# Half-row transposes in the projection's tiling, and the next columns' transposes at the head of a step

## The chip, the core and the metric

One core of a Trainium2 chip runs the whole program. The metric is device time in microseconds (us), the median of several runs; lower is better. The engines are TensorE (PE; its weight loads are shown apart as PEld), VectorE (DVE), ScalarE (ACT), GpSimd (POOL) and SyncE (SP), which here only issues DMAs.

## What is computed

An image x of 512 x 512 pixels with 64 channels goes through two layers of the same form. All data are fp32. Cut to what matters:

```python
def conv(x):                       # one layer; L = 512, H = 128 hidden channels
    xn = layernorm(x)              # over the 64 channels
    left = (xn @ Wl) * mask * sigmoid(xn @ Wlg)
    right = (xn @ Wr) * mask * sigmoid(xn @ Wrg)
    gate = sigmoid(xn @ Wog)
    # banded: out[i, j] = sum over d in -4..4 of left[i + d, i] * right[i + d, j], channel by channel
    out = banded_ingoing(left, right, 4)
    return (layernorm(out) * gate) @ Wo

for _ in range(2):
    x = x + conv(groupnorm(x))     # groupnorm: 32 groups, statistics over all pixels
```

(Biases are added too; they are left out here.)

## The kernel before, in words

Rows are cut into nine blocks of 64 rows that overlap by eight; columns into units of eight columns. A unit holds, on the 128 partitions, the 64 rows of a block twice: the lower 64 partitions have eight columns of the left half of the image, the upper 64 eight columns of the right half. A chunk is 16 units (JC = 128 columns in each half), and a layer has 18 chunks, so 288 units, plus five units of columns near the diagonal for `left`, early in the layer.

`layer` (L674) is one loop over steps t, and in a step each part works on another unit. Every call through `en` is kept in program order on its engine, so the order in which the loop writes things is the order in which each engine does them. In a step, in this order:

- GpSimd applies groupnorm's scale and shift to a unit some seven steps ahead (`affine`, L415; two operations, z<-z,ga and z<-z,gb).
- `gates` (L594): TensorE multiplies the stored transposed rows (zg) by the gate's weights, twice 64 rows by 448 columns; ScalarE takes the sigmoid into two gate tiles.
- `right` (L459), twice: `projected` (L447) multiplies the transposed unit zT by the weights into a tile of two PSUM banks, each matmul using 64 of the 128 rows of the array, with the two halves of the image in the two row tiles; ScalarE takes a sigmoid (sg), VectorE multiplies the two into RO.
- `inner_norm` (L424) of unit t+2 on GpSimd (z<-z,sti and z<-z,rs).
- `transposed` (L430) of unit t+1: four transposes of 128 x 128 into one PSUM bank, then ScalarE copies the bank to zT and SyncE stores zT to `later`, from where `recall` (L590) brings it back as zg some 30 steps on.
- `turned` (L613): eight transposes of 128 x 128 of the normed mix `on`, four into each of two banks; VectorE adds, multiplies by the gate and writes ZH.
- `biased` (L637) on GpSimd, then `end` (L643) of the step before: the output projection from ZH on TensorE, a VectorE addition into XR and the output's DMAs. In layer 0, `sums` (L662) accumulates the next groupnorm's statistics (acc).
- In every fourth step `solve` (L549): VectorE prepares var and rs, GpSimd works out the reciprocal roots by Newton steps, for four units to come.
- `norm` (L582): eight ScalarE activations from RO to `on`, of which there is one buffer.
- `mix` (L511), none, one or two times a step: 32 matmuls on 64 x 64 tiles into two banks; the banks are copied back into RO by ScalarE (first half) and ScalarE or VectorE (second half). Of 16 steps the first ten have 2, 1, 2, 2, 1, 2, 1, 2, 2, 1 mixes, the last six none (L695).

PSUM is shared out by two pools: `two_banks` (L131) has two buffers and serves `projected` and `mix`; `one_bank` (L128) has three buffers in layer 0 and four in layer 1 (L899) and serves transposes, gates and output. A user of a buffer waits until the one before it has been read out. zT has two buffers, sg two, z twelve.

Of the kernel before, what the change touches and what calls it, by code (L numbers as in the profile page):

```python
# [8 lines left out]
F32 = mybir.dt.float32  # L9
I32 = mybir.dt.int32  # L10
AF = mybir.ActivationFunctionType
ALU = mybir.AluOpType
# [4 lines left out]
P = 128  # L17
WIN = 4
NEAR = 2 * WIN + 1
S = 64  # L20
JC = 128
JW = 16
JU = 8
JQ = 4
NU = JC // JU
# [54 lines left out]
def tile_two_banded_layers(  # L80
# [8 lines left out]
    H = layers[0]["Wl"].shape[1]  # L89
    x, out = x[0], out[0]  # L90
# [22 lines left out]
    ident = const.tile([P, P], F32, name="ident")  # L113
# [14 lines left out]
    def one_bank():  # L128
        return ps.tile([P, 512], F32, tag="ps", name="bank")

    def two_banks():  # L131
        return ps2.tile([P, 1024], F32, tag="ps2", name="banks")
# [30 lines left out]
    def views(pack: bass.AP) -> dict:  # L163
        r, at = {}, 0
        for nm, n in PARTS:
            r[nm] = pack[:, at : at + n]
            at += n
        return r
# [184 lines left out]
    w = views(pack)  # L353
# [75 lines left out]

    def transposed(u: Unit):  # L430

        u.t = ztp.tile([P, JU // 2, P], F32, tag="zT", name="zT")
        pt = one_bank()
        for k in range(JU // 2):
            en.tensor.transpose(
                pt[:, k * P : (k + 1) * P],
                u.z[:, 2 * k : 2 * k + 2, :].rearrange("p j c -> p (j c)"), ident,
            )
        en.scalar.activation(u.t.rearrange("c k p -> c (k p)"), pt, AF.Identity, bias=1.0)
        if u.near is None:  # L440
            en.sync.dma_start(later[u.at], u.t)

    def place(k: int, e: int) -> int:

        return k // 2 * 4 + 2 * e + k % 2
# [147 lines left out]

    def gates(o: Out, w: dict):  # L594
        b = o.blk
        o.g = []
        pgs = [
            one_bank()[:, : 2 * JQ * b.m].rearrange("h (k p) -> h k p", p=b.m) for e in range(2)
        ]
        for e, pg in enumerate(pgs):  # L600
            part = slice(e * D, (e + 1) * D)
            en.tensor.matmul(
                pg, lhsT=w["gate"][part],
                rhs=o.t[part].rearrange("c k (e p) -> c (k e) p", e=2)[:, :, b.lo : b.hi],
                start=True, stop=True,
            )
        for pg in pgs:
            g = gp.tile([H, 2 * JQ * (S - WIN)], F32, tag="gate", name="gate")
            g = g[:, : 2 * JQ * b.m].rearrange("h (k p) -> h k p", p=b.m)
            en.scalar.activation(g, pg, AF.Sigmoid)  # L610
            o.g.append(g)

    def turned(o: Out, w: dict):  # L613

        b = o.blk
        for e in range(2):
            pt = one_bank()
            for k in range(JQ):
                en.tensor.transpose(
                    pt[:, k * P : (k + 1) * P], o.on[:, place(k, e), :], ident  # L620
                )
            zh = ZH[(2 * o.n + e) % len(ZH)]
            en.vector.scalar_tensor_tensor(
                zh[:, :, : b.m], pt.rearrange("h (k p) -> h k p", p=S)[:, :, b.lo : b.hi], w["ob"], o.g[e],
                ALU.add, ALU.mult,
            )

    def rows_of(v: bass.AP, o: Out, e: int):
        b, j = o.blk, e * LH + o.j
        return v[b.s + b.lo : b.s + b.hi, j : j + JU, :].rearrange("p (k t) c -> p k (t c)", t=2)  # L630
# [12 lines left out]
    def end(dst: bass.AP, o: Out, w: dict):  # L643
        m = o.blk.m
        po = one_bank().rearrange("i (j c) -> i j c", c=D)
        for k in range(JQ):
            for e in range(2):
                for n in range(2):

                    en.tensor.matmul(  # L650
                        po[n * S : (n + 1) * S, 2 * k + e, :],
                        lhsT=ZH[(2 * o.n + e) % len(ZH)][:, 2 * k + n, :], rhs=w["Wo"],
                        start=True, stop=True,
                    )
        f = o.xr[: S + m, :, 1 : 1 + 2 * D]
        en.vector.tensor_tensor(
            f, po[: S + m].rearrange("i (k t) c -> i k (t c)", t=2), f, ALU.add
        )
        for e in range(2):
            en.sync.dma_start(rows_of(dst, o, e), o.xr[e * S : e * S + m, :, 1 : 1 + 2 * D])  # L660
# [13 lines left out]
    def layer(src: bass.AP, dst: bass.AP, w: dict, stats: bool, then=None):  # L674
# [6 lines left out]
        for c in range(n_chunks):  # L681
            b, t0 = blocks[c // per], (c + 1) * NU
            for k in range(NU):
                t = c * NU + k
                units[t] = u = Unit(t, blk=b, j=c % per * JC + k * JU)
                j = k * JU if c % 2 == 0 else (JC + k * JU if k < own else JC - JW + (k - own) * JU)
                u.c = j

            for f in range(NU):
                o = outs[c * NU + LAG + f] = Out(  # L690
                    b, units[c * NU + (f + own) % NU], c % per * JC + f * JU
                )
# [9 lines left out]
        for n in range(0, NEAR * JQ, JU):  # L702
            t = 3 + n // JU * 2
# [3 lines left out]
        def inputs(t: int) -> list:  # L707
            return [d[t] for d in (units, lefts) if t in d]
# [22 lines left out]
        for t in range(min(loads), last_t + 3):  # L731
            if then and t == max(units) + 2:
                then()
            for u in loads.get(t, []):
                if u not in early:
                    load(src, u)
            if t + 2 in outs:
                recall(outs[t + 2])
            if t + 1 in outs:
                fetch(src, outs[t + 1], w, t + 1)  # L740
            for c, h in slabs.get(t, []):
                A[c, h] = take_left(c // per, h)

            for o in looks.get(t, []):
                if sto is None:
                    sto = sm.tile([P, NB // 2, 6], F32, tag="sto", name="sto"), []
                st, os = sto
                for k in range(JU // 2):
                    out_stats(o, st[:, len(os) * (JU // 2) :], k)
                os.append(o)  # L750

            for u in affines.pop(t, []):
                affine(u, en.vector if u.at < NU + 4 else en.gpsimd)
            if t % 4 == 3 and t > NU:
                then_affine = affines.pop(t + 1, [])
            if t in outs:
                gates(outs[t], w)

            todo = []
            for at, u in inners.get(t, []):  # L760
                key = (at + 2) // 4
                if key not in sti:
                    sti[key] = sm.tile([P, 3 * NB // 4, 6], F32, tag="sti", name="sti", bufs=3), []
                st, us = sti[key]
                n = len(us) * (JU // 2)
                u.mean = st[:, n : n + JU // 2, 1::3]
                todo += [(u, st[:, n : n + JU // 2, :], k) for k in range(JU // 2)]
                us.append(u)
            for v in todo[: len(todo) // 2]:
                inner_stats(*v)  # L770
            if t in units:
                for q in range(0, JU, JQ):
                    right(units[t], q, w)
            if t in lefts:
                for q in range(0, min(JU, NEAR * JQ - lefts[t].near), JQ):
                    left(lefts[t], q, w)
            for u in inputs(t + 2):
                inner_norm(u)
            for u in inputs(t + 1):
                transposed(u)  # L780
            if t in outs:
                turned(outs[t], w)
                biased(outs[t], w, stats)
            for v in todo[len(todo) // 2 :]:
                inner_stats(*v)
            if t - 1 in outs:
                end(dst, outs[t - 1], w)
            if stats and t - 2 in outs:
                sums(outs[t - 2], t - 2 == first_t, t - 2 == last_t)
            if t % 4 == 3:  # L790
                st, us = sti.pop((t + 5) // 4, (None, []))
                so, os = sto or (None, [])
                sto = None
                for u in then_affine:
                    affine(u, en.gpsimd)
                then_affine = []
                if us or os:
                    solve(w, us, os, st, so)
            if t + 1 in outs:
                norm(outs[t + 1])  # L800
            for n, (c, h0) in enumerate(mixes.get(t, [])):
                mix(c, A[c, h0 // HA], h0, [True, n + 1 < len(mixes[t])])
# [77 lines left out]
    ZH = [keep.tile([H, 2 * JQ, S], F32, name=f"ZH{i}") for i in range(4)]  # L880
# [9 lines left out]
    lp = ctx.enter_context(tc.tile_pool(name="lp", bufs=NA))  # L890
    wk = ctx.enter_context(tc.tile_pool(name="wk", bufs=3))
    onp = ctx.enter_context(tc.tile_pool(name="onp", bufs=1))
    gp = ctx.enter_context(tc.tile_pool(name="gp", bufs=2))

    next(one, None)
    nc.sync.dma_start(pack, spare)
# [35 lines left out]
```

## Time and profile before

| what | value |
|---|---|
| median of 3 runs | 5074.97 us (5073.14 to 5075.13) |
| the profiled execution | 5074.14 us, span 5072.3 us |
| granted TensorE clock in it | 0.978 |
| TensorE busy | 4496.1 us, 89% |
| VectorE, ScalarE, GpSimd busy | 3732.8, 3793.8 and 3826.9 us (74 to 75% each) |
| transposes of z, 128 x 128, 2344 in number | 390.6 us, 128.8 us idle ahead of them |
| transposes of on, 128 x 128, 4608 in number | 616.6 us, 14.7 us idle ahead of them |
| evictions to zT, 586 in number | 350.1 us, 597 ns each |

Each instruction is named by its output and inputs, such as bank<-ident,z for the transposes of z, banks<-pack,zT for the projection, banks<-RO,A for the mix, bank<-zg,pack for the gates and bank<-pack,ZH for the output projection. All of them carry the line of the one wrapper that records them (L362), so they are told apart by name. A number after an arrow is time in which the engine stood idle just before such instructions, with the engine that released it. An fp32 matmul is two records, a transpose one. Ends of matmuls are modelled, so it is the distance between starts that says what TensorE takes.

### The profile page before, as it was taken

How to read it: one execution, taken by the hardware profiler on the slowest of the kernel's cores; microseconds unless marked ns; L12 is line 12 of the kernel's file. 1: busy time of each engine (PE TensorE's matmuls, PEld its weight loads, DVE VectorE, ACT ScalarE, POOL GpSimd, SP SyncE). 2: the span in 40 equal slices, each digit the busy share in tenths (PEclk: the TensorE clock that was granted, in tenths of full speed). 3: DMA queues.
4: the chain of work that ended last, by engine and by line, in shares of the span. 5: the costliest groups of instructions: out<-in, count | busy, mean ns of one | idle time of the engine just before them, and what ended most of it. 6: DMA issues, size and time to landing. Idle time of an engine off the chain costs nothing.

```text
span 5072.3 us, 159784 instructions
## 1 busy us (share of the span) xinstructions
PE 4496.1 (89%) x60138; PEld 3714.8 (73%) x60138; DVE 3732.8 (74%) x9445; ACT 3793.8 (75%) x8328; POOL 3826.9 (75%) x4739
## 2 busy tenths in 40 slices
PE   1027999999999999999995599999999999999999
PEld 0015788888888888888873478888888888888886
DVE  6764677777777777777766467777777777777776
ACT  0013788888888888888884268888888888888888
POOL 0037888888888888888733598888888888888863
PEclk9988999999999999999997799999999999999999
DMA  7924666666666666666663456767676776777766
GB/s 317 400 58 125 176 194 197 195 195 193 198 196 195 194 194 197 196 194 198 189 171 102 106 176 201 202 198 202 200 205 201 202 203 200 202 204 204 204 182 173
DMA packets 905291, 981.45 MB, mean 193 GB/s; under 512 B 114210, under 2 KB 641608, under 8 KB 900168
## 3 DMA queue, kind: packets, MB, share of 16 engines
q1 hardware_dynamic: 897248, 948.49, 63.5%
q10 hardware_dynamic: 7272, 22.73, 1.1%
q8 instruction: 477, 7.82, 0.7%
q14 instruction: 294, 2.41, 0.2%
HBM read 658.42 MB, written 312.46 MB: 191 GB/s over the span
## 4 chain that ended last, share of the span: by engine, by line
PE 72%; POOL 9%; DMA 6%; DVE 4%; ACT 3%; issue 2%; SPq 2%; another core or an unknown queue 0%; ACTq 0%; POOLq 0%; DVEq 0%
PE banks L362 38%; PE bank L362 32%; POOL z L362 6%; ACT on L362 2%; DMA left_of<-nothing 2%; PE acc L362 2%; SPq L362 2%; DVE RO L362 1%; POOL XR L362 1%; DMA gn_x<-in_x_dram 1%; POOL rsqrt L362 1%; DVE ZH L362 1%; DMA XR<-mid_x 1%; DVE sto L362 1%; ACT gate L362 1%
## 5 line engine op out<-in xcount | busy, mean ns | idle before, releaser
L362 ACT ACTIVATE on<-RO,nm,rs 128x128 f32<-128x128 f32 x4608 | 1879.2, 495 | 172.4 <-PE bank L362 169.9
L362 PE MATMUL banks<-pack,zT 64*128 64x256 f32 x9360 | 1213.1, 389 | 137.0 <-ACT zT L362 76.6
L362 PEld LDWEIGHTS banks<-pack,zT 64*128 64x128 f32 x9360 | 967.2, 192 | 419.8 <-issue 180.4
L362 PE MATMUL banks<-RO,A 64*64 64x128 f32 x18432 | 1154.5, 277 | 15.6 <-DVE RO L362 15.4
L362 PEld LDWEIGHTS banks<-RO,A 64*64 64x64 f32 x18432 | 1082.4, 183 | 43.6 <-DVE RO L362 18.6
L362 DVE TENSOR_TENSOR RO<-banks,sg 128x512 f32<-128x512 f32 x1152 | 747.0, 681 | 258.8 <-ACT sg L362 258.0
L362 ACT ACTIVATE sg<-banks 128x512 f32<-128x512 f32 (+1 forms) x1188 | 682.7, 589 | 319.8 <-PE banks L362 208.0
L362 DVE COPY RO<-banks 128x512 f32<-128x512 f32 x360 | 248.9, 692 | 869.1 <-ACT RO L362 869.1
L362 DVE BATCH_NORM_STATS2 sto<-RO 128x6 f32<-128x256 f32 x2304 | 797.5, 411 | 1.2
L362 DVE SCALAR_TENSOR_TENSOR ZH<-bank,pack,gate 128x448 f32<-128x448 f32 (+1 forms) x1152 | 740.0, 682 | 37.6 <-ACT gate L362 36.3
L362 POOL TENSOR_TENSOR z<-z,gb 128x512 f32<-128x512 f32 x536 | 687.7, 1283 | 42.1
L362 POOL TENSOR_TENSOR z<-z,ga 128x512 f32<-128x512 f32 x536 | 687.5, 1283 | 0.1
L362 PE MATMUL bank<-zg,pack 64*128 64x448 f32 (+1 forms) x2304 | 657.4, 595 | 18.9 <-DVE ZH L362 15.8
L362 PE MATMUL bank<-pack,ZH 128*64 128x64 f32 x18432 | 663.5, 225 | 2.8 <-ACT zT L362 0.3
L362 ACT ACTIVATE gate<-bank 128x448 f32<-128x448 f32 (+1 forms) x1152 | 567.1, 542 | 126.6 <-PE bank L362 125.8
L362 PEld LDWEIGHTS bank<-pack,ZH 128*64 128x64 f32 x18432 | 584.0, 138 | 100.3 <-ACT zT L362 83.2
L362 POOL TENSOR_TENSOR z<-z,rs 128x512 f32<-128x512 f32 x586 | 618.0, 1055 | 45.9
L362 PE MATMUL bank<-ident,on 128*128 128x128 f32 x4608 | 616.6, 274 | 14.7 <-ACT gate L362 12.1
L362 POOL TENSOR_TENSOR z<-z,sti 128x512 f32<-128x512 f32 x586 | 623.8, 1065 | 0.0
L362 ACT COPY RO<-banks 128x512 f32<-128x512 f32 x792 | 441.2, 586 | 239.0 <-PE banks L362 237.8
L362 PEld LDWEIGHTS bank<-ident,on 128*128 128x128 f32 x4608 | 519.7, 141 | 74.0 <-ACT on L362 24.3
L362 POOL TENSOR_TENSOR XR<-XR,pack 120x512 f32<-120x512 f32 (+1 forms) x352 | 418.4, 1189 | 192.4 <-DMA XR<-mid_x 90.4
(137 smaller groups left out, 3927.6 us busy)
## 6 DMA issues: line engine op xcount, KB each, us to landing
later<-zT SPq DMA_DIRECT2D x576, 256.0 KB
A<-left_of SPq DMA_DIRECT2D x576, 256.0 KB
zg<-later SPq DMA_DIRECT2D x576, 256.0 KB
z<-in_x_dram SPq DMA_DIRECT2D x576, 128.0 KB
z<-mid_x SPq DMA_DIRECT2D x576, 128.0 KB
gn_x<-in_x_dram SPq DMA_DIRECT2D x16, 4096.0 KB
XR<-in_x_dram SPq DMA_DIRECT2D x448, 112.0 KB
mid_x<-XR SPq DMA_DIRECT2D x448, 112.0 KB
```

The costliest lines, as they stand in the source:

```text
L362: return lambda *a, **k: tc.keep_in_program_order(f(*a, **k))
```

## The change

Five things change, and nothing in the arithmetic.

1. `transposed` works on half rows: eight transposes instead of four, each of 64 partitions by 128 columns against a 64 x 64 part of the identity. The two halves of the partitions go to two different PSUM banks. For most units both come from one `two_banks` tile; for the first 17 units of a layer and the five near the diagonal they are two `one_bank` tiles.
2. Its eviction is a function of its own, `kept`: one activation over both banks (or two, for two tiles), which puts the halves together in zT, and the DMA to `later`.
3. Both are called for unit t+1 ahead of `gates` and `right` of step t, no longer after `right`.
4. `turned` works on half rows as well: sixteen transposes instead of eight, the halves in two banks, both evicted after the last transpose.
5. The gate is one tile of twice the size with one buffer, instead of two tiles with two, and ZH is indexed by half instead of by e.

```diff
     def transposed(u: Unit):
+        if u.near is None and u.at > NU:
+            u.pt = [two_banks().rearrange("c (n x) -> c n x", n=2)[:, :, : JU // 2 * S]]
+            halves = [u.pt[0][:, n] for n in range(2)]
+        else:
+
+            halves = [one_bank()[:, : JU // 2 * S] for n in range(2)]
+            u.pt = [h.unsqueeze(1) for h in halves]
+        for k in range(JU // 2):
+            for n in range(2):
+                part = slice(n * S, (n + 1) * S)
+                en.tensor.transpose(
+                    halves[n][:, k * S : (k + 1) * S],
+                    u.z[part, 2 * k : 2 * k + 2, :].rearrange("p j c -> p (j c)"),
+                    ident[part, part],
+                )
+
+    def kept(u: Unit):
         u.t = ztp.tile([P, JU // 2, P], F32, tag="zT", name="zT")
-        pt = one_bank()
-        for k in range(JU // 2):
-            en.tensor.transpose(
-                pt[:, k * P : (k + 1) * P],
-                u.z[:, 2 * k : 2 * k + 2, :].rearrange("p j c -> p (j c)"), ident,
-            )
-        en.scalar.activation(u.t.rearrange("c k p -> c (k p)"), pt, AF.Identity, bias=1.0)
+        to = u.t.rearrange("c k (n p) -> c n k p", n=2)
+        for n, pt in enumerate(u.pt):
+            en.scalar.activation(
+                to[:, n : n + pt.shape[1]], pt.rearrange("c n (k p) -> c n k p", p=S),
+                AF.Identity, bias=1.0,
+            )
         if u.near is None:
             en.sync.dma_start(later[u.at], u.t)
...
     def turned(o: Out, w: dict):
 
         b = o.blk
+        pts = [one_bank().rearrange("h (x p) -> h x p", p=S) for n in range(2)]
         for e in range(2):
-            pt = one_bank()
             for k in range(JQ):
-                en.tensor.transpose(
-                    pt[:, k * P : (k + 1) * P], o.on[:, place(k, e), :], ident
-                )
-            zh = ZH[(2 * o.n + e) % len(ZH)]
+                for n, pt in enumerate(pts):
+                    part = slice(n * S, (n + 1) * S)
+                    en.tensor.transpose(
+                        pt[:, e * JQ + k, :], o.on[part, place(k, e), :], ident[part, part]
+                    )
+        for n, pt in enumerate(pts):
             en.vector.scalar_tensor_tensor(
-                zh[:, :, : b.m], pt.rearrange("h (k p) -> h k p", p=S)[:, :, b.lo : b.hi], w["ob"], o.g[e],
-                ALU.add, ALU.mult,
+                ZH[(2 * o.n + n) % len(ZH)][:, :, : b.m], pt[:, :, b.lo : b.hi], w["ob"],
+                o.g[:, n], ALU.add, ALU.mult,
             )
...
             if t % 4 == 3 and t > NU:
                 then_affine = affines.pop(t + 1, [])
+            for u in inputs(t + 1):
+                transposed(u)
+                kept(u)
             if t in outs:
                 gates(outs[t], w)
...
             for u in inputs(t + 2):
                 inner_norm(u)
-            for u in inputs(t + 1):
-                transposed(u)
             if t in outs:
                 turned(outs[t], w)
...
-    gp = ctx.enter_context(tc.tile_pool(name="gp", bufs=2))
+    gp = ctx.enter_context(tc.tile_pool(name="gp", bufs=1))
```

More of the change, by code (lines that the diff above doesn't have):

```diff
@@ L595, in gates @@
         b = o.blk
[L596 to L599, printed above, removed]
+        n = 2 * JQ * b.m
+        pgs = [one_bank()[:, :n].rearrange("h (k p) -> h k p", p=b.m) for e in range(2)]
         for e, pg in enumerate(pgs):
@@ L606, in gates @@
             )
[L607 to L611, printed above, removed]
+        g = gp.tile([H, 4 * JQ * (S - WIN)], F32, tag="gate", name="gate")
+        for e, pg in enumerate(pgs):
+            en.scalar.activation(
+                g[:, e * n : (e + 1) * n].rearrange("h (k p) -> h k p", p=b.m), pg, AF.Sigmoid
+            )
+        o.g = g[:, : 2 * n].rearrange("h (x n p) -> h n x p", n=2, p=b.m)
     def turned(o: Out, w: dict):
         b = o.blk
+        pts = [one_bank().rearrange("h (x p) -> h x p", p=S) for n in range(2)]
         for e in range(2):
-            pt = one_bank()
             for k in range(JQ):
-                en.tensor.transpose(
-                    pt[:, k * P : (k + 1) * P], o.on[:, place(k, e), :], ident
-                )
-            zh = ZH[(2 * o.n + e) % len(ZH)]
+                for n, pt in enumerate(pts):
[4 more added lines that the diff above has]
+        for n, pt in enumerate(pts):
             en.vector.scalar_tensor_tensor(
-                zh[:, :, : b.m], pt.rearrange("h (k p) -> h k p", p=S)[:, :, b.lo : b.hi], w["ob"], o.g[e],
-                ALU.add, ALU.mult,
+                ZH[(2 * o.n + n) % len(ZH)][:, :, : b.m], pt[:, :, b.lo : b.hi], w["ob"],
+                o.g[:, n], ALU.add, ALU.mult,
             )
@@ L651, in end @@
                         po[n * S : (n + 1) * S, 2 * k + e, :],
-                        lhsT=ZH[(2 * o.n + e) % len(ZH)][:, 2 * k + n, :], rhs=w["Wo"],
+                        lhsT=ZH[(2 * o.n + n) % len(ZH)][:, e * JQ + k, :], rhs=w["Wo"],
                         start=True, stop=True,
```

## The prediction

> **What bounds the kernel now.** I read the page's busy slices first, then the table by stretches, then the timeline of TensorE and GpSimd inside one stretch.
>
> ```profile
> PE 4496.1 (89%) x60138; PEld 3714.8 (73%) x60138; DVE 3732.8 (74%) x9445; ACT 3793.8 (75%) x8328; POOL 3826.9 (75%) x4739
> ...
> PE   1027999999999999999995599999999999999999
> ```
>
> TensorE is full in every slice except the set-up and the two starts of a layer; the other four engines stand near 75%. But an average mixes stretches. A chunk of 16 steps (124.9 us in layer 0, 121.1 in layer 1) has ten steps with mixes and six without. The table by stretches, for one chunk of layer 0 (us; busy PE, PEld, DVE, ACT, POOL; clock, DMA share, GB/s):
>
> ```profile
> 1937.69:2016.37 78.68, 78.68 (x1170) 67.95 (x1169) 52.87 (x136) 63.78 (x136) 70.99 (x80) 1.00 0.67 190
> 2016.37:2035.41 19.04, 18.37 (x242) 15.22 (x240) 18.19 (x49) 16.34 (x36) 9.73 (x17) 1.00 0.67 195
> 2035.41:2052.90 17.49, 17.28 (x244) 13.87 (x240) 15.08 (x39) 16.62 (x40) 16.94 (x17) 1.00 0.72 212
> ```
>
> Mix steps: TensorE 78.68 of 78.68. The first three steps without a mix: VectorE 18.19 of 19.04. The last three: GpSimd 16.94 of 17.49. So three engines take turns, and TensorE is only just slower than GpSimd in the last stretch. The timeline there (start, length), TensorE and then GpSimd:
>
> ```profile
> 2035.41 1.02 PE L362 MATMUL bank<-zg,pack 64*128 64x448 f32 x4
> 2036.27 1.89 PE L362 MATMUL banks<-pack,zT 64*128 64x256 f32 x16
> 2038.14 0.66 PE L362 MATMUL bank<-ident,z 128*128 128x128 f32 x4
> 2038.64 1.04 PE L362 MATMUL bank<-ident,on 128*128 128x128 f32 x8
> 2039.63 1.15 PE L362 MATMUL bank<-pack,ZH 128*64 128x64 f32 x32
> 2040.61 0.64 PE L362 MATMUL acc<-XR 120*64 120x65 f32 x16
> 2041.18 1.02 PE L362 MATMUL bank<-zg,pack 64*128 64x448 f32 x4
> ```
> ```profile
> 2031.38 0.29 POOL L362 TENSOR_TENSOR rsqrt<-rs 128x64 f32<-128x64 f32 x1 [4.56 <-DVE rs L362]
> ...
> 2035.92 1.05 POOL L362 TENSOR_TENSOR z<-z,sti 128x512 f32<-128x512 f32 x1
> 2037.05 1.04 POOL L362 TENSOR_TENSOR z<-z,rs 128x512 f32<-128x512 f32 x1
> ```
>
> GpSimd's normalisation ends at 2038.09 and the transposes of z start at 2038.14: they wait for it. What covers that wait today are the gates and the projection of the same step, issued ahead (2035.41 to 2038.14). In the next two steps it is the same (z at 2044.02 and 2049.90, 5.88 us apart: GpSimd's 2.13 + 1.14 + 2.61 for norm, bias, affine).
>
> **What the Trainium skill says.** "TensorEngine Tiling (Array Packing)", Key Properties: changing the tiling mode drains the array. The trace agrees: the last pair of the projection takes 0.306 instead of its 0.216, and the first transpose 0.165 instead of 0.109. "TensorE: Matmul & The Clock Gate", section LDWEIGHTS: a load costs by columns, not by rows. The trace differs, and decides:
>
> ```profile
> L362 PEld LDWEIGHTS banks<-pack,zT 64*128 64x128 f32 x9360 | 967.2, 192 | 419.8 <-issue 180.4 <-ACT zT L362 96.8 <-DVE RO L362 50.3
> ...
> L362 PEld LDWEIGHTS bank<-ident,on 128*128 128x128 f32 x4608 | 519.7, 141 | 74.0 <-ACT on L362 24.3 <-ACT gate L362 20.8 <-ACT RO L362 14.1
> ```
>
> The same 128 columns read 51 ns longer in a 64-row tile; single records agree (an exposed load delays the first matmul by 0.104 at the gates, 0.056 at z). The same page, Part 3: loads overlap if their row groups differ. At the gates both halves' loads start 7 ns apart, so two run together.
>
> **The change, part by part.** Times per step, from the single records.
> (1) Tiling. Now, from the end of a mix to the output projection: gates 0.86 (0.104 exposed load, two pairs at 0.376), projection 1.82, z 0.49, the on-transposes 0.97: 4.14. After: z first, 0.104 + 4p, gates 0.75, projection 1.73, on 8p + 0.09, where p is the time of a pair of half transposes: 2.67 + 12p. One change of mode (0.09 + 0.056) is gone, and the gates' load hides under z. p is not in the trace. Below: the load alone, 0.104; above: 0.121, the pair pitch of the mix (3.87 us for 32 pairs), which streams the 128 columns that cost 0.109 untiled. Were both loads serial, 0.21, but the gates speak against it. I take 0.115: 4.05, a gain of 0.09 (0.22 to 0.02).
> (2) z moves into two_banks, and the built order shows that after a mix the projection's first bank is the one that z just left, so it waits for zT. ScalarE: copy of the mix from 0.12 to 0.71 after the mix, zT to about 1.34, seen at 1.40. TensorE would be there at 0.10 + 4 x 0.115 + 0.75 = 1.32. Cost about 0.06 to 0.08, leaving a gain of 0.03 per mix step, 10 x 0.03 = 0.3 per chunk (1.5 to -0.5). In layer 1 a step with one mix lasts 7.25, less than the 7.55 after which ScalarE ends its eight activations on; there zT comes some 0.2 later, in three steps: 0.6.
> (3) z is moved ahead of gates and projection. In mix steps z has been ready for long (3.4 to 11 us for most; 1.6 to 2.5 in the first two steps). In the last three steps the cover of 2.7 us is taken off. Layer 0: z cannot start before 2038.13; then the whole step follows it, 5.69 - 0.09 = 5.60, to 2043.73; z ready at 2043.97; 2049.57, ready at 2049.84; then 2055.44, where the mix step begins today at 2052.90: 2.5 late. GpSimd gets nothing back for it: its own chain starts at VectorE's rs (2031.4), which ends an unbroken VectorE run from the last mix. Step 1 gains nothing in these six steps, as VectorE and GpSimd set them. ScalarE's sum is 5.9 per step (zT 0.6, gates 0.95, sg 1.05, on 3.25), so zT behind on adds about 0.2. Layer 0: 2.5 + 0.2 - 0.3 = 2.4 per chunk. Layer 1: the same recurrence with 5.22 per step gives 2.5; but there the mix stands waiting for VectorE 1.3 in the next step, which swallows that much; the step after has z 1.7 before its use against 2.7 of lost cover and so waits 0.4; with 0.6 of (2), less 0.3: 1.9.
> (4) Half rows in the first 17 units: two activations (128x256 at 0.381) for one of 0.597, 0.17 each, ScalarE half idle there: nothing, 4 us if not. turned now evicts after all sixteen instead of eight: at worst 0.5 late for VectorE, which is read a step later: nothing. gp with one double tile: the gate's sigmoid waits for the ZH of the step before, done by then. SP: later is issued 2.7 earlier and still ahead of the output; the queue behind it waits for zT a shorter time. GpSimd's order is unchanged. The two ends: steps without a projection save about 0.12 in 28 steps per layer, 7 together. Starts of the layers: zT now stands ahead of sg in ScalarE's queue, where today sg waits 96 us for left_of and zT 53 us for later; zT being ready when the wait ends could save 3 in some of eight places, and its own wait now holds sg: between -25 and +15, taken -10.
>
> Sum: 16 chunks with such stretches per layer: 16 x 2.4 + 16 x 1.9 = 69, less 7 and 10: 52. On the profiled execution (span 5072.3, 1.8 around it, time 5074.1) 5126; that one stands 0.8 under the median of the runs, so 5127.
>
> **The rivals.** A, faster: p at its lower bound and the starts at theirs. Then a mix step gains 0.15 after its wait, 1.5 per chunk, against 2.2 left of step 3: +0.7 x 32 = 22, minus 7, minus 25, minus what the earlier z saves VectorE's stretch (gates there wait 0.4 to 0.6 for ZH, twice; z would fill it): 20 if VectorE follows. In all -30: 5045. It decides once step 3 costs less than ten gains of step 1, that is below 0.15 per mix step. For it: the gates' loads run in parallel; against: VectorE is full in that stretch, and the mix never reaches 0.109. B, no change: a gain of 0.18 per mix step instead of 0.03 (p near its lower bound, zT early), the rest as forecast: 52 - 32 x 10 x 0.15 = +4, 5079. C, clearly slower: zT's eviction becomes the bound in every mix step: ScalarE's queue puts it after the copy, and each 0.1 beyond costs 32 x 10 x 0.1 = 32; at 0.3 more: 5222.
>
> **How the numbers follow.** Forecast 0.56 (own range 5095 to 5165), A 0.19, B 0.10, C 0.15. The range 5055 to 5200 leaves out about half of A and a third of C. This kernel's measurement can tell about 0.2%, 10 us. Faster 0.19, within 0.2% 0.11 (B and the edge), slower 0.70.
>
> **What would show it.** Right: in the last three steps without a mix, TensorE idle 2 to 4 us ahead of the first z, released by GpSimd, and nothing between z and the end of the step; waits of TensorE for z up by about 70 us or more; VectorE's stretch unchanged; pairs of halves 0.105 to 0.121 apart; the projection after a mix held by zT for under 0.1. Wrong: chunk periods at or below 124.9 and 121.1; pairs below 0.10 or above 0.15; or GpSimd's solve starting earlier in the chunk, which would mean that VectorE's run was shortened.

## The result and the profile after

| | before | after |
|---|---|---|
| median, same series of runs | 5073.14 us | 5099.26 us (5094.57 to 5104.45) |
| ratio | | 1.0055, 95% interval 1.004 to 1.0069 |
| the profiled execution | 5074.14 us | 5100.56 us, span 5098.6 us |
| granted clock in it | 0.978 | 0.927 |

The changed kernel is 26 us slower; 52 were forecast. Direction and range held, but the sum did not: two of its terms were wrong by about a hundred and by about seventy-five, with opposite signs. The page after, its busy line of TensorE and the busy slices:

```profile
PE 4296.7 (84%) x67090; PEld 3572.6 (70%) x67090; DVE 3696.4 (72%) x9445; ACT 3793.5 (74%) x8372; POOL 3821.5 (75%) x4739
...
PE   1025899999999999999984479999999999999998
```

TensorE has 200 us less to do and the kernel is slower. The slices that differ are at the start (0258 where it was 0279) and in the middle, where layer 1 starts (4479 where it was 5599). So one looks there first.

The places where a mix begins are easy to find in the trace (banks<-RO,A), and they cut a layer into comparable stretches. "Mix stretch" is from a chunk's first mix to its last, "gap" from there to the first mix of the next chunk, both medians over the steady chunks; worked out from the starts of the records, in us:

| kernel | median | first mix | mix stretch of chunk 0 | layer 0: mix, gap | last mix of layer 0 to first of layer 1 | layer 1: mix, gap |
|---|---|---|---|---|---|---|
| before | 5073 | 460.8 | 57.5 | 80.6, 44.4 | 280.2 | 76.3, 44.8 |
| after | 5099 | 477.9 | 67.9 | 76.4, 47.1 | 299.5 | 72.8, 46.7 |
| start_old | 5045 | 461.0 | 58.1 | 76.4, 47.1 | 278.7 | 72.9, 46.7 |
| nomix_old | 5049 | 477.7 | 68.0 | 77.3, 44.7 | 301.1 | 75.3, 43.6 |
| both_old | 4986 | 458.6 | 58.1 | 77.8, 43.9 | 279.1 | 73.7, 44.8 |
| on_halves | 5016 | 461.2 | 58.1 | 79.5, 44.2 | 282.0 | 74.3, 43.7 |
| serial_on | 5218 | 480.6 | 65.7 | 79.1, 48.3 | 302.7 | 75.1, 47.7 |
| move_only | 5318 | 481.2 | 61.2 | 81.9, 50.5 | 301.1 | 77.7, 48.0 |
| tiling_only | 5459 | 461.8 | 64.1 | 86.1, 50.1 | 277.9 | 82.5, 50.4 |
| start_bank | 5083 | 475.9 | 60.0 | 76.4, 47.1 | 297.3 | 72.8, 46.7 |
| late_head | 4960 | 459.4 | 57.5 | 76.7, 44.1 | 279.8 | 74.3, 43.6 |

The ledger of the two profiled executions, from the first two rows and the starts behind them: layer 0 up to the first mix of its second chunk +31.6; its next sixteen chunks -21.3; from there to the first mix of layer 1 +20.2, and to the first of its second chunk +14.9; sixteen chunks -16.6; the last chunk -2.4. Sum 26.4. Steady chunks became faster, by 1.3 and 1.0 us each in the mean (1.5 and 1.6 by the medians of the table, since single chunks of layer 1 differ), where 2.4 and 1.9 slower were forecast. The two starts of a layer lost 67, where 10 of gain were forecast.

Inside a steady chunk of layer 0, the table by stretches of the changed kernel (us; busy PE, PEld, DVE, ACT, POOL; clock, DMA share, GB/s), cut as in the prediction:

```profile
1955.16:2029.68 74.52, 74.52 (x1282) 63.69 (x1280) 53.44 (x136) 63.84 (x137) 68.35 (x78) 1.00 0.73 202
2029.68:2051.64 21.96, 17.09 (x282) 14.37 (x280) 20.21 (x55) 17.65 (x40) 13.87 (x22) 0.98 0.74 209
2051.64:2068.94 17.30, 17.30 (x281) 14.20 (x279) 12.52 (x30) 15.44 (x36) 15.71 (x15) 0.93 0.51 145
```

Mix steps 78.68 to 74.52; the next three steps 19.04 to 21.96, with TensorE busy only 17.09 of them; the last three as long as before. The idle time is one wait. TensorE and then GpSimd there:

```profile
2046.91 0.64 PE L362 MATMUL acc<-XR 120*64 120x65 f32 x16
2051.16 0.69 PE L362 MATMUL banks<-ident,z 64*128 64x64 f32 x8 [3.62 <-POOL z L362]
2051.64 1.81 PE L362 MATMUL bank<-zg,pack 64*128 64x448 f32 x4
2053.24 2.32 PE L362 MATMUL banks<-pack,zT 64*128 64x256 f32 x16
...
2057.54 0.47 PE L362 MATMUL banks<-ident,z 64*128 64x64 f32 x8
```
```profile
2044.41 0.29 POOL L362 TENSOR_TENSOR rsqrt<-rs 128x64 f32<-128x64 f32 x1 [4.34 <-DVE rs L362]
...
2048.94 1.05 POOL L362 TENSOR_TENSOR z<-z,sti 128x512 f32<-128x512 f32 x1
2050.07 1.04 POOL L362 TENSOR_TENSOR z<-z,rs 128x512 f32<-128x512 f32 x1
...
2055.91 1.04 POOL L362 TENSOR_TENSOR z<-z,rs 128x512 f32<-128x512 f32 x1
```

GpSimd ends the normalisation at 2051.11, and z starts at 2051.16 after 3.62 of idleness; the gates and the projection, which used to fill that time, now follow it. GpSimd's roots begin 14.7 after the last mix (2044.41 less 2029.68), 15.0 before the change (2031.38 less 2016.37): VectorE's stretch is nearly unchanged. All this is as forecast, but for one thing: the z of the next step has no wait. GpSimd has it ready at 2056.95 (2055.91 and 1.04), about as forecast, but TensorE comes to it only at 2057.54, because its own step took 6.38 and not 5.60. The step after the wait ran at a lower granted clock (the value before the DMA share):

```profile
2051.16:2053.24 2.08, 2.08 (x12) 1.27 (x14) 0.00 (x0) 0.60 (x1) 2.08 (x2) 0.50 0.07 20
```

At 0.50, z takes 0.48 here and the gates 1.60, where a mix step has 0.30 and 0.96 (below). The clock records of the traces show 0.50 for 3.4 or 6.8 us in the gap of each of the 32 steady chunks of the changed kernel, and in none of them in before, nomix_old and late_head, which do not have this long wait. By this, the lost cover costs twice: the wait, and the slow step behind it. No run separates the two; in this chunk the second z starts 0.59 after it is ready.

A mix step, on TensorE and then ScalarE:

```profile
1971.22 0.46 PE L362 MATMUL banks<-ident,z 64*128 64x64 f32 x8
1971.52 0.97 PE L362 MATMUL bank<-zg,pack 64*128 64x448 f32 x4
1972.48 2.00 PE L362 MATMUL banks<-pack,zT 64*128 64x256 f32 x16
1974.31 0.66 PE L362 MATMUL bank<-ident,on 64*128 64x64 f32 x16
1974.90 0.28 PE L362 MATMUL bank<-pack,ZH 128*64 128x64 f32 x2
```
```profile
1971.34 0.58 ACT L362 COPY RO<-banks 128x512 f32<-128x512 f32 x1 [0.76 <-PE banks L362]
1971.83 0.60 ACT L362 ACTIVATE zT<-banks 128x512 f32<-128x512 f32 x1
```

From start to start: z 0.30 (was 0.49), gates 0.96 (0.86), projection 1.83 (1.82), on 0.59 (0.97). The sum is 3.68 instead of 4.14, and a step with two mixes is 9.10 instead of 9.56. The projection starts 0.05 after zT ends (1971.83 + 0.60): the wait for zT that was forecast is there; its size follows from both_old below. What was not forecast is how short the transposes are: eight pairs of on take 0.438 from first to last start, which is 0.062 a pair. The records of their loads (busy, mean ns of one | idle before):

```profile
L362 PEld LDWEIGHTS bank<-ident,on 64*128 64x128 f32 x9216 | 413.9, 139 | 126.3 <-ACT gate L362 40.0 <-issue 17.3 <-DVE XR L362 8.0
```

### The profile page after: what moved, and what is told of

Read it like the earlier page. It is cut to its first block, busy times and chain, and to the rows that moved or that the text cites. A ratio compares the mean times of both kernels' runs of the same rounds, so it can differ in the third digit from the quotient of the medians.

```text
span 5098.6 us, 172846 instructions
## 1 busy us (share of the span) xinstructions
PE 4296.7 (84%) x67090; PEld 3572.6 (70%) x67090; DVE 3696.4 (72%) x9445; ACT 3793.5 (74%) x8372; POOL 3821.5 (75%) x4739
## 4 chain that ended last, share of the span: by engine, by line
PE 65%; POOL 8%; DMA 7%; DVE 7%; ACT 6%; SPq 3%; issue 3%; ACTq 0%; another core or an unknown queue 0%; POOLq 0%; DVEq 0%
PE banks L362 40%; PE bank L362 23%; POOL z L362 4%; ACT on L362 3%; SPq L362 3%; POOL rsqrt L362 3%; DMA left_of<-nothing 2%; PE acc L362 2%; DVE RO L362 2%; DVE ZH L362 2%; DMA gn_x<-in_x_dram 1%; DVE sti L362 1%; ACT gate L362 1%; DMA zg<-later 1%; ACT sg L362 1%
## 5 line engine op out<-in xcount | busy, mean ns | idle before, releaser
L362 PE MATMUL banks<-pack,zT 64*128 64x256 f32 x9360 | 1347.5, 411 | 122.8 <-DVE RO L362 75.7
L362 PEld LDWEIGHTS banks<-pack,zT 64*128 64x128 f32 x9360 | 1006.2, 201 | 529.0 <-ACT zT L362 316.5
L362 DVE TENSOR_TENSOR RO<-banks,sg 128x512 f32<-128x512 f32 x1152 | 768.5, 686 | 547.2 <-ACT sg L362 542.5
L362 PE MATMUL bank<-zg,pack 64*128 64x448 f32 (+1 forms) x2304 | 691.1, 600 | 22.2 <-DVE ZH L362 22.0
L362 DVE BATCH_NORM_STATS2 sti<-z 128x6 f32<-128x128 f32 x2344 | 546.6, 281 | 0.9 <-DMA z<-mid_x 0.5
L362 PEld LDWEIGHTS bank<-ident,on 64*128 64x128 f32 x9216 | 413.9, 139 | 126.3 <-ACT gate L362 40.0
```

The source lines that it names most:

```text
L362: return lambda *a, **k: tc.keep_in_program_order(f(*a, **k))
```

## The experiments

All kernels are compared with the kernel before in the same runs, whose median was 5070 to 5073.

**start_old**: the changed kernel, with the old order and the old whole transposes in the steps of a layer that have no outputs. In the diffs, `whole` is the `transposed` of the kernel before, and it stands where that stood.

```diff
-            for u in inputs(t + 1):
+            ahead_of_gates = t in outs
+            for u in inputs(t + 1) if ahead_of_gates else []:
                 transposed(u)
                 kept(u)
...
             for u in inputs(t + 2):
                 inner_norm(u)
+            for u in inputs(t + 1) if not ahead_of_gates else []:
+                whole(u)
```

> The changed kernel, but in the steps of a layer that have no output yet (the first 30) the next columns are transposed whole, 128 x 128, and after the projection, as before the change. Theory 'order': the two starts lose 32 and 34 us because z at the head of a step loses the projection as cover for GpSimd's normalisation, and because without gates nothing covers the copy to zT; then the first mix stands again at about 461 and the first gates at about 539, both layers give back 66 together, and the time is 5033 (5027 to 5040). Rival 'clock': the starts are slower because the granted clock was 0.55 to 0.6 there instead of 0.7; then the first gates stay at 560 or later and the time is 5085 to 5099.

Measured: 5044.59 (ratio to before 0.9942, 0.9927 to 0.9957). The first mix stands at 461.0 and the start of layer 1 is as short as before; 55 of the expected 66 came back, since the gap after chunk 0, 43.8 where it was 39.8, still has the new order in its last steps. So most of the losses of the starts come from the order, and the changed kernel without them is faster than the kernel before. That the clock was not the cause is shown by nomix_old too: with other granted clocks in its first slices its first mix stands at 477.7, as in the changed kernel. The slices of the changed kernel and of nomix_old:

```profile
PEclk6556999999999999999997699999999999999999
```
```profile
PEclk9977999999999999999997699999999999999999
```

What the order does in the steps with columns near the diagonal is read from TensorE and GpSimd of the changed kernel:

```profile
399.31 3.78 PE L362 MATMUL banks<-pack,zT 64*128 64x256 f32 x16 [3.71 <-DVE RO L362]
407.13 0.69 PE L362 MATMUL bank<-ident,z 64*128 64x64 f32 x8 [4.04 <-POOL z L362]
```
```profile
402.17 1.07 POOL L362 TENSOR_TENSOR sg<-sg,pack 128x512 f32<-128x512 f32 x1 [18.80 <-ACT sg L362]
403.87 1.07 POOL L362 TENSOR_TENSOR sg<-sg,pack 128x512 f32<-128x512 f32 x1 [0.64 <-ACT sg L362]
404.90 1.05 POOL L362 TENSOR_TENSOR z<-z,sti 128x512 f32<-128x512 f32 x1
406.03 1.04 POOL L362 TENSOR_TENSOR z<-z,rs 128x512 f32<-128x512 f32 x1
```

In `left`, GpSimd multiplies sg by the mask after that step's projection, and the normalisation of z is queued behind it. With z at the head of the next step TensorE has to wait for that whole chain, 4.04 us here, before it may issue the next projection. In the kernel before, the next projection is issued first:

```profile
392.22 2.16 PE L362 MATMUL banks<-pack,zT 64*128 64x256 f32 x16 [1.34 <-DVE sg L362]
394.50 0.66 PE L362 MATMUL bank<-ident,z 128*128 128x128 f32 x4
```

**nomix_old**: the same edit for the six steps of a chunk without mixes.

```diff
+            ahead_of_gates = t not in outs or t in mixes
```

> The changed kernel, but in the six steps of a chunk that have no mix (and have outputs) the next columns are transposed whole and after the projection, as before the change; the starts are left as changed. Theory 'cover': the stretch from the last mix of a chunk to the first of the next, 44.5 and 44.8 before and 47.1 and 46.7 now, is longer because the first z of the last three steps waits for GpSimd; it goes back to 44.5 and 44.8, 15 x 2.6 + 15 x 1.9 = 68 less: 5031. Rival 'backlog': the mix steps became 4 us shorter, so VectorE and GpSimd bring that much more unfinished work into the stretch, and it stays at 46 to 47 wherever z stands: 5090 to 5099.

Measured: 5049.46 (0.9955, 0.994 to 0.9969). The gap goes back to 44.7 and 43.6, so 'cover' holds and 'backlog' falls for the gap. But the mix stretch grows from 76.4 to 77.3 and from 72.8 to 75.3, so that 50 came back and not 68: part of the wait returns in the first mix steps. In the second of them, z waits 1.1 in layer 0 and 1.6 in layer 1 for GpSimd, in the mean of the steady chunks.

**both_old**: both edits, z by halves at the head only in steps that have outputs and mixes.

```diff
+            ahead_of_gates = t in outs and t in mixes
```

> The changed kernel with both edits: z by halves at the head only in steps that have outputs and mixes, otherwise whole and after the projection. If 'order' and 'cover' both hold the mix stretches keep their gain (80.5 to 76.4 and 76.3 to 72.8), and the rest is as before the change: 5099 - 66 - 68 = 4965 (4955 to 4980). If 'clock' and 'backlog' hold, 5080 or more.

Measured: 4985.94 (0.9831, 0.9817 to 0.9846), within 21 of the expectation and just outside its range. What is missing is in the first mix steps, as the timeline of TensorE shows:

```profile
2013.76 0.46 PE L362 MATMUL banks<-ident,z 64*128 64x64 f32 x8 [0.32 <-POOL z L362]
2014.06 0.97 PE L362 MATMUL bank<-zg,pack 64*128 64x448 f32 x4
2014.87 1.94 PE L362 MATMUL banks<-pack,zT 64*128 64x256 f32 x16
2016.64 0.66 PE L362 MATMUL bank<-ident,on 64*128 64x64 f32 x16
...
2019.58 3.95 PE L362 MATMUL banks<-RO,A 64*64 64x128 f32 x64 [0.73 <-DVE RO L362]
2024.47 0.46 PE L362 MATMUL banks<-ident,z 64*128 64x64 f32 x8 [0.94 <-POOL z L362]
```

Two more z at the head come before GpSimd is done with them. The first of these steps follows no mix, so no copy of a mix stands ahead of zT on ScalarE: gates take 0.81 and the projection 1.77 from start to start, where a step behind a mix takes 0.96 and 1.83. By this comparison the wait for zT costs 0.2 in a mix step.

**on_halves**: the kernel before with the new `turned`, `gates` and `end`, and the old z.

```diff
 def turned(o: Out, w: dict):
+        pts = [one_bank().rearrange("h (x p) -> h x p", p=S) for n in range(2)]
...
+                    en.tensor.transpose(
+                        pt[:, e * JQ + k, :], o.on[part, place(k, e), :], ident[part, part]
+                    )
```

> The kernel before, with only the transposes of on by halves (and the gate tile and ZH that go with it); z is transposed whole, after the projection. Theory 'pairs': a pair of half transposes takes 0.062, so the group of on takes 0.59 instead of 0.97; one more change of mode between z and on costs about 0.15; 0.23 is left per mix step, 10 x 32 x 0.23 = 74: 4999 (4985 to 5015), with the mix stretches 2.3 shorter each. Rival 'mode': changes of mode cost 0.3 or more each, and the gain of the pairs is mostly eaten: 5045 to 5073. The prediction's price of a pair, 0.115, would make it slower: about 5130.

Measured: 5016.06 (0.9889, 0.9872 to 0.9905), just outside the range. The prediction's price of a pair falls; 'pairs' holds in its sign. In the trace z goes from 0.493 to 0.587 in both layers, but on goes from 0.967 to 0.758 in layer 0 and to 0.643 in layer 1. In layer 1, then, 0.23 is left, as 'pairs' had it, and the change of mode between z and on costs 0.15 (0.587 + 0.643 against 0.49 + 0.59, the whole z of before and the halves of after). In layer 0 only 0.12 is left. TensorE of layer 0, the copy of z on ScalarE beside it, and TensorE of layer 1:

```profile
1928.86 0.72 PE L362 MATMUL bank<-ident,on 64*128 64x64 f32 x16
1929.62 1.15 PE L362 MATMUL bank<-pack,ZH 128*64 128x64 f32 x32
```
```profile
1928.97 0.60 ACT L362 ACTIVATE zT<-bank 128x512 f32<-128x512 f32 x1
```
```profile
4058.13 0.71 PE L362 MATMUL bank<-ident,on 64*128 64x64 f32 x16
4058.77 1.15 PE L362 MATMUL bank<-pack,ZH 128*64 128x64 f32 x32
```

In layer 0 the output projection starts 0.05 after the copy of z has ended, in 256 of the layer's steps. There `one_bank` has three buffers, and the output takes the bank that z has left; with the four of layer 1 it does not. So the 0.12 is a wait for a bank, which shows because the halves of on are done sooner. Half transposes still pay fully only where no whole ones stand between them and the projection.

**serial_on**: the changed kernel, with the half transposes of on in another order.

```diff
-        for e in range(2):
-            for k in range(JQ):
-                for n, pt in enumerate(pts):
-                    part = slice(n * S, (n + 1) * S)
+        for n, pt in enumerate(pts):
+            part = slice(n * S, (n + 1) * S)
+            for e in range(2):
+                for k in range(JQ):
```

> The changed kernel, with the sixteen half transposes of on in another order: the eight of the lower partitions, then the eight of the upper ones, so that neighbours no longer use different halves of the rows. Theory 'side by side': a pair takes 0.062 because its two halves run together, so one alone takes about the same or more, and the group grows from 0.59 to 1.05 or more: 0.46 in 320 mix steps and in about half of the 192 others, 5099 + 150 to 190 = 5250 to 5290. Rival 'small': a half costs 0.031 by itself, because it streams 64 columns and loads 64 rows, and the order makes no difference: 5099.

Measured: 5217.92 (1.0285, 1.0269 to 1.03), below the range: the group of on grows from 0.590 to 0.889, not to 1.05. The single records of one group say why (starts in ns after the first; a sign + joins two within 10 ns):

```
after      0+7  56+63  119+124  181+187  242+248  305+313  368+375  430+438
serial_on  0  56  118  180  242+249  307  365+369  428+431  492  555  617  679  741
```

In the same rows one half follows the other after 0.062; in the changed kernel a pair does. So a half alone costs as much as a pair, and the second half of a pair is free. In serial_on the first transpose of the second bank, known by its load that waits for that bank, already starts at 249, beside the fifth of the first: it did not wait for the three halves that stand before it in the program. Three such overlaps save 3 x 0.062 of the 15 x 0.062 that a strict order would take, which leaves the 0.741. 'Side by side' holds, 'small' falls. The Trainium skill, "TensorE: Matmul & The Clock Gate", Part 3, says that small matmuls with different row groups run concurrently, and the trace agrees. It also says there that matmuls are strictly in order in their starts; these starts differ from that, 249 ahead of 307, and the measurement decides. The groups of the changed kernel and of serial_on (busy, mean ns of one | idle before):

```profile
L362 PE MATMUL bank<-ident,on 64*128 64x64 f32 x9216 | 441.2, 224 | 33.2 <-ACT gate L362 28.2 <-DVE XR L362 3.1
```
```profile
L362 PE MATMUL bank<-ident,on 64*128 64x64 f32 x9216 | 606.2, 226 | 11.7 <-ACT gate L362 5.4
```

The mean of one is the same, 224 and 226 ns; only the busy sum, which counts overlap once, tells that 165 us more pass.

**move_only**: the kernel before with z's whole transposes at the head.

```diff
+            for u in inputs(t + 1):
+                transposed(u)
             if t in outs:
                 gates(outs[t], w)
...
-            for u in inputs(t + 1):
-                transposed(u)
```

> The kernel before, with z's whole transposes and their eviction moved to the head of the step in every step; no half rows. Theory 'order': the move alone brings all of the losses and none of the gains: 66 at the two starts, 68 in the stretches without mixes (44.5 to 47.1, 44.8 to 46.7), and in each of 320 mix steps one more change of mode, 0.2 to 0.3 by the run with halves of on alone, and about 0.05 of waiting for zT: 80 together. 5073 + 214 = 5287 (5250 to 5315). Rival: in mix steps the place of z makes no difference: 5073 + 134 = 5207.

Measured: 5317.77 (1.0478, 1.0462 to 1.0493), 3 above the range. The first mix at 481.2 and the 301.1 between the layers are close to those of the changed kernel (477.9 and 299.5): the losses of the starts belong to the move. The mix stretch is 1.3 longer (forecast 2 to 3), which is 0.15 in each of its nine steps, again the price of one more change of mode; the gap of layer 0 6.1 longer (forecast 2.6): there, with steps that are longer than those of the changed kernel, the delay is not made up; that this is the whole reason is not shown.

**tiling_only**: the changed kernel with z's halves behind the projection.

```diff
-            for u in inputs(t + 1):
-                transposed(u)
-                kept(u)
             if t in outs:
                 gates(outs[t], w)
...
             for u in inputs(t + 2):
                 inner_norm(u)
+            for u in inputs(t + 1):
+                transposed(u)
+                kept(u)
```

> The changed kernel with z's halves and their eviction put back behind the projection in every step, still in two_banks. Theory 'buffer': the third user of two_banks in a step waits until the first tile of the projection has been read out, sg 0.59 and RO 0.69 after it, some 0.6 after the projection's end; the step's part is then 0.86 + 1.73 + 0.6 + 0.30 + 0.59 = 4.08 instead of 4.14, and the starts and the stretches without mixes are as before the change: 5055 (5035 to 5085). Rival 'free': VectorE is early enough and nothing waits: 0.65 less in each of 320 mix steps, 4865.

Measured: 5459.36 (1.0763, 1.0745 to 1.0781), far beyond both. The group of z's transposes (busy, mean | idle before, released by) says which wait it is:

```profile
L362 PE MATMUL banks<-ident,z 64*128 64x64 f32 x4336 | 254.6, 234 | 700.0 <-DVE RO L362 508.8 <-POOL z L362 114.2 <-POOL rs L362 46.1
```

The kind was right and the size was not. From the projection's start to z it takes 2.61 in some mix steps and 3.0 to 3.4 in most, not the 1.73 + 0.6 expected: VectorE has other work queued ahead of the RO that frees the bank, in one such step statistics from 2102.00 on, and the RO only at 2103.70, after a projection that began at 2101.51; z starts at 2104.52. With z in `two_banks` the tiling of z pays only together with its move: 5459 for the tiling at the old place, 5318 for the move alone, 5099 for both.

**start_bank**: the changed kernel, with one_bank tiles for z until the outputs begin.

```diff
-        if u.near is None and u.at > NU:
+        if u.near is None and u.at > NU + 15:
```

> The changed kernel, with z's halves in two one_bank tiles for the first 32 units of a layer instead of the first 17; two_banks serves z only after that. Steps without outputs leave one_bank free. Theory 'bank': in the ten mix steps that have no output yet, 67.9 long from first to last mix instead of 57.5, the projection's first bank is the one that z has just left, and no gates stand between to cover the copy to zT; with other banks the stretch falls to 61 (as in the run with the move alone, 61.2), 7 less in each layer: 5099 - 14 = 5085 (5078 to 5092). The first mix stays at 478. Rival: two activations for one make the copy itself later, and the projection waits for zT's own contents as before: no change, 5095 to 5104.

Measured: 5082.88 (1.0025, 1.0014 to 1.0035), as 'bank' had it. In the mix steps without outputs nothing stands between z and the projection. The changed kernel first, then start_bank:

```profile
484.14 0.69 PE L362 MATMUL banks<-ident,z 64*128 64x64 f32 x8 [2.28 <-POOL z L362]
485.52 3.79 PE L362 MATMUL banks<-pack,zT 64*128 64x256 f32 x16 [0.69 <-ACT zT L362]
```
```profile
488.72 0.46 PE L362 MATMUL bank<-ident,z 64*128 64x64 f32 x8
489.02 2.32 PE L362 MATMUL banks<-pack,zT 64*128 64x256 f32 x16
```

The projection waits 0.69 for the copy of z out of the bank that it needs, and not at all where z uses another pool.

**late_head**: as both_old, but also old in the first two mix steps.

```diff
+            ahead_of_gates = t in outs and t in mixes and t % NU > 1
```

> As the run with both edits, but z also stands whole and behind the projection in the first two mix steps of a chunk, where GpSimd is only 1.4 to 2.4 ahead. In the run with both edits the trace shows TensorE waiting there 0.3, 0.9 and, for VectorE, 0.7 in a chunk. Theory 'cover': the first two waits go, two times 0.45 of the tiling's gain is given up: 0.4 less per chunk, 13: 4973 (4960 to 4985). Rival: GpSimd sets the pace through the first three mix steps whatever the order, the wait moves on to the third: 4986 to 5000.

Measured: 4960.44 (0.9778, 0.9763 to 0.9792), the fastest kernel of the study: 112 less than before, 139 less than the change as it came. 'Cover' holds in layer 0: in its chunk at 2005 to 2024 the first two mixes start without a wait, that for VectorE included. In layer 1 the rival has a part, as one chunk shows:

```profile
3756.51 3.94 PE L362 MATMUL banks<-RO,A 64*64 64x128 f32 x64 [0.49 <-DVE RO L362]
...
3768.30 0.46 PE L362 MATMUL banks<-ident,z 64*128 64x64 f32 x8 [0.82 <-POOL z L362]
```

The first mix waits for VectorE, and the wait for GpSimd has moved on to the third step with mixes. Half of the 112 does not need the move at all: on_halves alone was 56 faster than before.

## Why the prediction was right in sign and wrong in its steps

Step by step, forecast and measured:

- Step 1, the price of a pair, was the first failure: "p is not in the trace. Below: the load alone, 0.104". Measured 0.062 (seven steps of a pair from 0 to 430 ns in the records above). The lower bound was no bound. A load of 0.104 was read where it stood exposed, at the gates; in a stream of transposes the next loads run under other work. Nor did the load of the gates stand for that of a half transpose: that the same 128 columns read longer in 64 rows holds for the projection's weights (192 ns), but the halves read 139, as the whole ones read 141. And the upper bound and the value taken came from the mix, which streams 128 columns in each 64 x 64 tile, where a half transpose streams 64: the identity that is streamed was halved as well, as the diff showed (`ident[part, part]`). Twelve pairs at 0.053 less make 0.64. Two smaller items went the other way: the exposed load of the gates and the drain were expected to save 0.1 each on gates and projection, and these two measured 0.96 and 1.83, which has the wait for zT in it. The net gain was 0.46 in most mix steps (0.33 in those of layer 1 with one mix) instead of 0.03.
- Step 2, the wait for zT through the shared bank: right in kind, but 0.2 a mix step (both_old) instead of 0.06 to 0.08: the shorter z brings TensorE to the projection sooner, while ScalarE still copies the mix ahead of zT. It failed where no gates stand between z and the projection, in the ten mix steps before the first output. There it costs 0.8 a step (start_bank: 7.9 less in layer 0 and 8.1 in layer 1, over ten steps), which was not priced at all.
- Step 3, the lost cover ahead of z: right in place and releaser, and near in size. By the medians the gap grew by 2.7 and 1.9; the forecast was 2.5 plus 0.2 in layer 0, and 2.5 less 1.3 plus 0.4 in layer 1 (its sum of 1.9 has terms of steps 1 and 2 in it). nomix_old took the growth away. The path to the size was wrong, though: each of the three steps was to follow GpSimd at full speed, while the trace has one wait of 3.62 and then a step at half the granted clock, for which the prediction has no term. That the size still came out near is in part luck.
- Step 4, the starts: "between -25 and +15, taken -10", measured +67. This is the same mechanism as in step 3, not applied there: only ScalarE's queue was looked at, not GpSimd's chain from `left` to the normalisation. start_old gives back 55 of the 67, move_only shows that it belongs to the move, and start_bank the part of the bank (16 of it).
- The sum: forecast 69 - 7 - 10 = 52. Measured: chunks -37.9, starts +66.7, end -2.4, which is 26.4. The slower time was thus right by luck: two errors that cancelled. Rival A had the mechanism of the chunks (cheap pairs outweigh the lost cover), and failed by the starts.

Of the signs named ahead, the idle time before the first z, VectorE's stretch and TensorE's waits for z (301.6 in the two groups below, 125.1 before) came as told; the chunk periods and the pairs answered "wrong", and both pointed at step 1. The projection was held by zT for more than the 0.1 that was told, which points at step 2.

```profile
PE banks L362 <- POOL z L362: 154.1, 62, 5.0
PE bank L362 <- POOL z L362: 147.5, 34, 31.1
```

What stays open: whether a half alone is cheaper than a whole by its 64 streamed columns or by its 64 rows (a half with 128 streamed columns was not tried); why the gap of move_only grows by 6.1 and not by 2.7 was not pursued, nor how much of the 0.15 for a change of mode in on_halves is drain and how much an exposed load; how much of the longer gap is the wait itself and how much the half clock behind it; and whether z by halves in two `one_bank` tiles, left at its old place, would keep the cheap pairs without any of the move's costs, which no run tried.

## What to carry to other kernels

When a step is moved ahead of others, list every stretch of the program in which it runs, the starts and ends too, and ask in each what used to run while its input was made; here the move paid at most in eight steps of sixteen, and with z by halves at the head only there, and on by halves everywhere, the kernel was 2.2% faster than before the change. Look at the granted clock behind each new wait of TensorE. Price an operation by the shape that it streams and loads, and take no lower bound from a place where it stands exposed. Where a sum comes out small against its terms, the terms are what has to be checked in the trace after: the right total said nothing here.

## What was not expected of the hardware

- Half transposes (64 rows, 64 streamed columns) follow each other after 0.062 us in the same rows, and a pair in different rows takes the same 0.062, against 0.109 for a whole one of 128 x 128.
- A transpose in the upper rows started up to three places ahead of its turn, beside one in the lower rows (serial_on: 249 ns, where the fifth of the lower ones had just started).
- The loads of half transposes (64 rows, 128 columns) read 139 ns and those of whole ones 141, while the projection's weights, 64 rows and 128 columns too, read 192 to 201.
- Behind the wait of 3.62 us the granted clock stood at 0.50 for 3.4 us; such a stretch, of 3.4 or 6.8 us, came in all 32 steady chunks of the changed kernel and in none of the kernel before.
- The granted clock of the first four slices was 0.5 to 0.6 in one execution and 0.7 to 0.9 in another, and the first mix started at the same time (477.9 in the changed kernel, 477.7 in nomix_old).
